# A graph layer with an expert layer behind it: chunks of a range summed together, an expert's first layer in pairs of blocks

## The chip, the cores and the metric

The kernel runs on one core of a Trainium2 chip. The time is the device time of one execution in microseconds (us); less is better. A core has engines that run side by side: TensorE (PE in the profile, with its weight loads as PEld), VectorE (DVE), ScalarE (ACT), GpSimd (POOL) and SyncE (SP), and 16 DMA engines. Each engine takes its own instructions in order; where one needs what another made, it waits for a semaphore.

## The reference

There are 6250 nodes with 256 features and 106,250 edges, sorted by their destination `dst`. Cut to what matters, it is

```python
deg = maximum(segment_sum(ones, dst), 1); norm = deg ** -0.5
# graph layer
h = norm * (layernorm(x) @ W.T + b)
x = x + segment_sum(h[src], dst) * norm
# expert layer, on the layernorm of the new x
scores = layernorm(x) @ Wg.T + bg              # 8 experts
top2, idx = top_k(scores, 2); p = softmax(top2)
for e in range(8):
    hid = relu(xn @ W1[e].T + b1[e])           # 256 -> 1024
    y = hid @ W2[e].T + b2[e]                  # 1024 -> 256
    x = x + combine[:, e] * y                  # combine holds p where idx is e
```

So every edge reads one row of 256 features at an address that is data, rows are summed by destination, and each node then goes through two of eight experts.

## The kernel before

**Start.** `gnn_ffn` (L1354) loads indices and x, and makes helper tiles. A value `bad` tells whether the edges are ordered well enough; L1422 loads it as `flag`, and `tc.If(flag == 0)` (L1423) runs `in_order`, its `Else` runs `any_order`. With the given data `in_order` runs. It first counts degrees and writes a table of scaled rows to memory (`ftable`, 128 rows at a time, each row 1 KB: a high and a low half in f16). This takes the first 93 us of the span.

**Main loop** (L816 to 832). The edges are 831 chunks of 128 (`NC`). A window is a run of successive chunks whose destinations lie within 128 nodes; there are 150, 110 of them of four or five chunks. Step s of the loop issues, for all engines, in this order:

- `gather(s + AHEAD)` (L391, DMA at L394): GpSimd starts an indirect DMA that brings the 128 source rows of a chunk six steps ahead (`AHEAD = 6`) into one of 24 buffers (`ROWS`).
- `mask(s + MASKS)` (L398, L401): VectorE makes a 128x128 matrix of ones and zeros that tells which edge goes to which node, six steps ahead, in one of nine buffers.
- `add_up(s)` (L403, L408): TensorE multiplies mask and rows (f16, 512 columns) and adds into the window's sum `ps` in PSUM (two buffers). It waits for the mask and for the row's DMA.
- The tasks planned for step s. `join(w)` (L474, L482 and L485 on VectorE, copies at L490 on ScalarE) adds the window's sum, one step after its last chunk, to what earlier windows left for the same nodes. A tile of 128 nodes is complete at step `FINAL[t]`, mostly 17 chunks after the one before. Then, at fixed steps counted from `s = FINAL[t] + 1`: `turn_sum` (s+2, L492), `linear` (s+4, L501, matmul at L505), `route` (s+5 and following, L508 to 599: residual at L513, layernorm, top two, softmax, positions `pos` at L592), `scatter` (L601, DMA at L603), which sends each row to the queues of its two experts by two indirect DMAs on GpSimd, at the positions that VectorE worked out. From s+16+LATE on `fetch`: `choose` (L618 to 657, VectorE) picks the expert with most rows waiting, `load_first` and `load_second` (L659 to 675) let SyncE load its weights (1152 and 1028 KB) and 256 of its rows.
- `next_piece(s)` (L792): one piece of the expert step that is on. There are 16 pieces of a full step of 256 rows: eight times `up` (L695 to 703: two matmuls in the code into `ph`, then ScalarE's relu with bias) and eight times `down` (L705 to 717: two matmuls into `py`; every fourth has VectorE add the bias, L715, and SyncE store the result). A second piece goes in at every fourth step when the experts are behind. `turn_rows` (matmuls at L690, copy at L692) brings the next step's rows into place.

The order is written out by hand (`tc.manual_schedule()`): each engine's queue holds its instructions in the order in which the loop names them. So GpSimd's scatters stand between its gathers, and a gather behind a scatter goes out only when VectorE has worked out where the scattered rows go.

In the trace each f32 matmul of the code is two records: `up` and `down` have four records a piece (1792 of L701 for 448 pieces, 1728 of L711 for 432).

**Tail** (L833 to 875). The remaining pieces, `read_back` (L773, indirect DMAs on GpSimd that bring each node's two results), `add_in` (L781) and stores. A last branch (L905) is for rows that no usual step took.

Of the kernel before, what the change touches and what calls it, by code (L numbers as in the profile page):

```python
# [19 lines left out]
P = 128  # L20
# [29 lines left out]
AHEAD = 6  # L50
UP = 2.0 ** 8
UP2 = 2.0 ** 11
MASKS = 6
ROWS = 24
# [44 lines left out]
BASE = [WINDOWS[w][0] for w in WINDOW]  # L99
FINAL = [max(chunks[-1] for n0, chunks in WINDOWS if n0 < (t + 1) * P) for t in range(NT)]  # L100
# [33 lines left out]
def in_order(ctx: ExitStack, tc: tile.TileContext, g: Shared):  # L134
# [240 lines left out]
    rows, masks, sums = {}, {}, {}  # L375
# [15 lines left out]
    def gather(c):  # L391
        nonlocal last_pool
        rows[c] = rowpool.tile([P, 2 * D], F16, name="rows")
        last_pool = nc.gpsimd.indirect_dma_start(  # L394
            out=rows[c], out_offset=None, in_=table[:, :],
            in_offset=bass.IndirectOffsetOnAxis(ap=g.src[:, c:c + 1], axis=0))

    def mask(c):  # L398
        masks[c] = work.tile([P, P], F16, name="mask", bufs=MASKS + 3)
        r = (P - BASE[c] % P) % P  # L400
        nc.vector.tensor_scalar(masks[c], g.col_b[:, r:r + P], g.rel[:, c:c + 1], None, op0=OP.is_equal)  # L401

    def add_up(c):  # L403
        w = WINDOW[c]
        chunks = WINDOWS[w][1]
        if c == chunks[0]:
            sums[w] = psp.tile([P, 2 * D], F32, name="ps")
        nc.tensor.matmul(sums[w], masks.pop(c), rows.pop(c), start=(c == chunks[0]), stop=(c == chunks[-1]))  # L408
# [37 lines left out]
    def inputs_scored(t0, t1):  # L446
        xT = turned_inputs.pop(t0)
        for t in range(t0, t1):
            px = psp.tile([P, NE], F32, name="ph")
            for k in range(2):  # L450
                nc.tensor.matmul(px, xT[:, k, (t - t0) * P:(t - t0 + 1) * P], wg[:, k, :],  # L451
                                 start=(k == 0), stop=(k == 1))
            nc.scalar.activation(xg[:, t, :], px, AF.Copy)
# [241 lines left out]
    def up(step, b):  # L695
        f = steps[step]
        w1 = f["w1"]
        n = rows_of(step)
        ph = psp.tile([P, FT], F32, name="ph")
        for k in range(2):  # L700
            nc.tensor.matmul(ph[:, :n], w1[:, k * H + b * P:k * H + (b + 1) * P], f["xT"][:, k, :n],  # L701
                             start=(k == 0), stop=(k == 1))
        nc.scalar.activation(f["hid"][:, b, :n], ph[:, :n], AF.Relu, bias=w1[:, 2 * H + b:2 * H + b + 1])  # L703

    def down(step, i):  # L705
        f = steps[step]
        a = i // 4
        if i % 4 == 0:
            f["py"] = psp.tile([P, D], F32, name="py")
        for b in (2 * (i % 4), 2 * (i % 4) + 1):  # L710
            nc.tensor.matmul(f["py"], f["hid"][:, b, a * P:(a + 1) * P], f["w2"][:, b * D:(b + 1) * D],  # L711
                             start=(b == 0), stop=(b == HB - 1))
        if i % 4 == 3:
# [6 lines left out]
        if i == 4 * rows_of(step) // P - 1:  # L720
            del steps[step]

# [36 lines left out]
    all_sent = FINAL[NT - 1] + 1 + 19  # L759
# [32 lines left out]
    def next_piece(s):  # L792
# [6 lines left out]
        if turned == step or (ahead and cur >= (12 if s < NC else 14)):  # L799
# [7 lines left out]
        if cur < HB:  # L807
            up(step, cur)
        else:
            down(step, cur - HB)  # L810
        cur += 1
        if cur == HB + 4 * rows_of(step) // P:
# [3 lines left out]
    with tc.manual_schedule():  # L816
        with rowp as rowpool:
            for c in range(AHEAD):
                gather(c)
            for c in range(MASKS):  # L820
                mask(c)
            for s in range(NC):
                if s + AHEAD < NC:
                    gather(s + AHEAD)
                if s + MASKS < NC:
                    mask(s + MASKS)
                add_up(s)
                for fn, args in tasks.pop(s, []):
                    fn(*args)
                next_piece(s)  # L830
                if s % 4 == 0 and earliest.get(done + 1, NC) <= s:
                    next_piece(s)
        with tc.tile_pool(name="ftail", bufs=2) as pool:  # L833
            s = NC
# [15 lines left out]
            while done < USUAL or tasks or len(plan) > 1 or asked < 2 * allowed or pend:  # L850
                for fn, args in tasks.pop(s, []):
                    fn(*args)
                if s > all_sent:
# [6 lines left out]
                    if loaded1 < min(chosen, done + (cur >= HB) + 3):  # L860
# [3 lines left out]
                next_piece(s)  # L864
# [26 lines left out]
            def more(step):  # L891

                some = some_left("some")
                with tc.If(nc.values_load(some[0:1, 0:1], min_val=0, max_val=1) > 0):
                    run(fetch(step))
                    turn_rows(step)
                    for b in range(HB):
                        up(step, b)
                    for i in range(8):
# [455 lines left out]
def gnn_ffn(ctx: ExitStack, tc: tile.TileContext, x, srcT, dstT, low, gW, gb, Wg, bg, W1, W2, out):  # L1355
# [67 lines left out]
    with tc.If(flag == 0) as cmp:  # L1423
        in_order(tc, g)
    with cmp.Else():
        any_order(tc, g, dstT)
# [43 lines left out]
```

## Time and profile before

| | |
|---|---|
| runs | 2164.18, 2155.74, 2160.90 us; median 2160.9 |
| profiled execution | 2166.43 us, of which the span in the profile is 2164.6 |
| mean granted TensorE clock | 0.803 |
| PE busy | 1379.5 us (64%), 6246 matmuls |
| DVE busy | 882.9 us (41%), 4681 instructions |
| ACT busy | 400.9 us (19%), 903 |
| POOL busy | 998.2 us (46%), 1082 |
| DMA | 320.09 MB, 148 GB/s; POOL's queue 20.8% and SP's 22.6% of the 16 engines' span |
| degrees and table | 0 to 93 us |
| main loop | 93 to about 1936 us, 2.2 us a step |
| tail | about 1936 us to the end |

Busy time is summed over an engine's instructions; issuing DMAs, waiting and branching don't count. A line of the groups gives source line, engine, operation, what it writes and reads, the count, busy time, the mean of one in ns, and the idle time of the engine just before, with what ended most of it. "remote" as a releaser is another core or a queue that the trace doesn't know; "issue" is time in which the engine waited for nothing that the profile shows.

### The profile page before, as it was taken

How to read it: one execution, taken by the hardware profiler on the slowest of the kernel's cores; microseconds unless marked ns; L12 is line 12 of the kernel's file. 1: busy time of each engine (PE TensorE's matmuls, PEld its weight loads, DVE VectorE, ACT ScalarE, POOL GpSimd, SP SyncE). 2: the span in 40 equal slices, each digit the busy share in tenths (PEclk: the TensorE clock that was granted, in tenths of full speed). 3: DMA queues.
4: the chain of work that ended last, by engine and by line, in shares of the span. 5: the costliest groups of instructions: out<-in, count | busy, mean ns of one | idle time of the engine just before them, and what ended most of it. 6: DMA issues, size and time to landing. Idle time of an engine off the chain costs nothing. (4 is left out here: it accounts for less than half of the span.)

```text
span 2164.6 us, 22195 instructions
## 1 busy us (share of the span) xinstructions
PE 1379.5 (64%) x6246; PEld 1001.8 (46%) x6246; DVE 882.9 (41%) x4681; ACT 400.9 (19%) x903; POOL 998.2 (46%) x1082
## 2 busy tenths in 40 slices
PE   5144557746677675665765766677576657577885
PEld 5033335534444454444544544445355435455664
DVE  8313434324435253443534335343343344344442
ACT  3511112111112121121211112111111112121222
POOL 1265463543544545354453544535454544414563
PEclk9996668877878788778877777878788868877898
DMA  5542253443343534344353443534353434526774
GB/s 202 203 157 77 61 174 108 153 144 103 133 156 113 174 114 162 118 136 152 111 166 117 147 143 112 176 109 157 130 173 117 168 128 152 206 93 219 235 252 164
DMA packets 116822, 320.09 MB, mean 148 GB/s; under 512 B 22388, under 2 KB 63560, under 8 KB 102344
## 3 DMA queue, kind: packets, MB, share of 16 engines
q1 hardware_dynamic: 64444, 175.27, 22.6%
q0 software_dynamic: 51568, 142.67, 20.8%
q8 instruction: 53, 0.87, 0.2%
q14 instruction: 89, 0.73, 0.1%
q10 hardware_dynamic: 668, 0.55, 0.1%
HBM read 269.01 MB, written 49.39 MB: 147 GB/s over the span
## 5 line engine op out<-in xcount | busy, mean ns | idle before, releaser
L394 POOL DMA_INDIRECT rows<-ftable,src x831 | 788.1, 948 | 260.1 <-issue 198.1
L711 PE MATMUL py<-w,hid 128*128 128x256 f32 x1728 | 529.7, 432 | 187.2 <-issue 157.9
L701 PE MATMUL ph<-xT,w 128*128 128x256 f32 (+1 forms) x1792 | 518.7, 424 | 160.4 <-ACT xT L692 97.7
L711 PEld LDWEIGHTS py<-w,hid 128*128 128x128 f32 x1728 | 368.2, 219 | 285.5 <-issue 185.2
L701 PEld LDWEIGHTS ph<-xT,w 128*128 128x128 f32 x1792 | 363.0, 215 | 268.9 <-ACT xT L692 117.7
L408 PE MATMUL ps<-rows,mask 128*128 128x512 f16 x831 | 355.7, 444 | 164.7 <-DMA rows<-ftable,src 59.0
L603 POOL DMA_INDIRECT fhq<-h,posi x98 | 98.0, 1000 | 731.8 <-DVE pos L592 533.2
L703 ACT ACTIVATE hid<-ph,w 128x256 f32<-128x256 f32 (+1 forms) x448 | 207.6, 465 | 628.4 <-PE ph L701 229.0
L401 DVE TENSOR_SCALAR mask<-col_b,rel 128x128 f16<-128x128 bf16 x831 | 203.3, 256 | 168.6 <-remote 73.5
L482 DVE SCALAR_TENSOR_TENSOR rolled<-rolled,keep,ps 128x256 f32<-128x256 f32 x149 | 71.2, 478 | 365.4 <-remote 160.7
L408 PEld LDWEIGHTS <-mask 128*128 128x128 f16 x831 | 92.8, 113 | 225.9 <-DVE rolled L485 78.2
L490 ACT ACTIVATE whole<-rolled 32x256 f32<-32x256 f32 (+2 forms) x156 | 64.6, 414 | 674.4 <-DVE rolled L485 621.5
L513 DVE SCALAR_TENSOR_TENSOR xr<-pt,norm,xr 128x256 f32<-128x256 f32 x49 | 23.6, 482 | 271.9 <-remote 162.1
L505 PE MATMUL pt<-gw,uT 128*128 128x264 f32 x196 | 65.6, 465 | 93.3 <-issue 55.8
L773 POOL DMA_INDIRECT yb<-fyq,rowat x98 | 94.2, 962 | 64.2 <-issue 22.3
L715 DVE TENSOR_TENSOR y<-py,w 128x256 f32<-128x256 f32 x108 | 45.5, 422 | 188.9 <-PE py L711 97.8
L505 PEld LDWEIGHTS pt<-gw,uT 128*128 128x128 f32 x196 | 41.0, 221 | 115.1 <-issue 66.3
L690 PE MATMUL px<-ident,xs 128*128 128x128 f32 x216 | 50.1, 356 | 47.4 <-issue 35.8
L451 PE MATMUL ph<-wg,xT 128*128 128x8 f32 x196 | 35.5, 307 | 67.0 <-ACT xT L443 44.4
L451 PEld LDWEIGHTS ph<-wg,xT 128*128 128x128 f32 x196 | 34.4, 259 | 83.7 <-ACT xT L443 55.1
L690 PEld LDWEIGHTS px<-ident,xs 128*128 128x128 f32 x216 | 37.9, 188 | 71.0 <-issue 56.0
L485 DVE SCALAR_TENSOR_TENSOR rolled<-ps,rolled 128x256 f32<-128x256 f32 x150 | 63.6, 424 | 5.2
(176 smaller groups left out, 1010.8 us busy)
## 6 DMA issues: line engine op xcount, KB each, us to landing
w<-in_W SPq DMA_DIRECT2D x56, 1152.0 KB
w<-in_W SPq DMA_DIRECT2D x56, 1028.0 KB
fyq<-y SPq DMA_DIRECT2D x108, 128.0 KB
xs<-fhq SPq DMA_DIRECT2D x52, 256.0 KB
rows<-ftable,src POOLq DMA_INDIRECT x831
fyq<-zero SPq DMA_DIRECT2D x28, 256.0 KB
out<-xr POOLq DMA_DIRECT2D x11, 512.0 KB
xr<-in_x SPq DMA_DIRECT2D x6, 896.0 KB
```

The costliest lines, as they stand in the source:

```text
L394: last_pool = nc.gpsimd.indirect_dma_start(out=rows[c], out_offset=None, in_=table[:, :], in_offset=bass.IndirectOffsetOnAxis(ap=g.src[:, ...
L401: nc.vector.tensor_scalar(masks[c], g.col_b[:, r:r + P], g.rel[:, c:c + 1], None, op0=OP.is_equal)
L408: nc.tensor.matmul(sums[w], masks.pop(c), rows.pop(c), start=(c == chunks[0]), stop=(c == chunks[-1]))
L451: nc.tensor.matmul(px, xT[:, k, (t - t0) * P:(t - t0 + 1) * P], wg[:, k, :], start=(k == 0), stop=(k == 1))
L482: nc.vector.scalar_tensor_tensor(new, rolled, keeps[kept[w]], ps[:, 0:D], op0=OP.mult, op1=OP.add)
L505: nc.tensor.matmul(pl, uT[:, k, :], gw[:, k, :], start=(k == 0), stop=(k == 1))
L603: s = nc.gpsimd.indirect_dma_start(out=hq[:, :], out_offset=bass.IndirectOffsetOnAxis(ap=ixs[t][:, j:j + 1], axis=0), in_=h2s[t], in_offse ...
L690: nc.tensor.transpose(px[:, k, a * P:(a + 1) * P], f["xs"][:, a, k * P:(k + 1) * P], g.ident)
L701: nc.tensor.matmul(ph[:, :n], w1[:, k * H + b * P:k * H + (b + 1) * P], f["xT"][:, k, :n], start=(k == 0), stop=(k == 1))
L703: nc.scalar.activation(f["hid"][:, b, :n], ph[:, :n], AF.Relu, bias=w1[:, 2 * H + b:2 * H + b + 1])
L711: nc.tensor.matmul(f["py"], f["hid"][:, b, a * P:(a + 1) * P], f["w2"][:, b * D:(b + 1) * D], start=(b == 0), stop=(b == HB - 1))
L773: r = nc.gpsimd.indirect_dma_start(out=yb, out_offset=None, in_=yq[:, :], in_offset=bass.IndirectOffsetOnAxis(ap=where[:, t, j:j + 1], axi ...
```

## The change

**Sums of a group.** A window's chunks are split into groups of at most five (`GATHERS`; 195 groups: 144 of four chunks, 51 of five). The rows of a group share a tile of five places, in six buffers (`ROWS = 6`); its masks share a tile, in three buffers. `add_up` now takes a whole group, one step after the group's last chunk, and its matmuls go from the last chunk to the first. `join` and all that is counted from `FINAL` come one step later.

**Masks.** `mask(s)` is made at step s, no longer six steps ahead, and waits until its chunk's rows have landed (`after`). The matmuls no longer wait for the rows' DMAs themselves (`free_order`), only for the masks. `AHEAD` goes from 6 to 8.

**Experts.** `up` takes two blocks: four matmuls into one PSUM tile of two halves, then two ScalarE operations. `down` takes four matmuls at a time. `next_piece` is called at even steps, and at s % 8 == 1 when behind, so that the rate of matmuls stays. `inputs_scored` gathers two tiles' scores in one PSUM tile and copies them at once. In the tail `next_piece` is called every second step, which starts at NC + 1.

**The other path apart.** `If`/`Else` becomes two `If`s, with `any_order` first.

```diff
-AHEAD = 6
+AHEAD = 8
-MASKS = 6
-ROWS = 24
+GATHERS = 5
+ROWS = 6
...
+def groups():
+
+    found = []
+    for n0, chunks in WINDOWS:
+        parts = -(-len(chunks) // GATHERS)
+        for i in range(parts):
+            found.append(chunks[i * len(chunks) // parts:(i + 1) * len(chunks) // parts])
+    return found
...
     def gather(c):
         nonlocal last_pool
-        rows[c] = rowpool.tile([P, 2 * D], F16, name="rows")
+        k, i = IN_GROUP[c]
+        if i == 0:
+            rows[k] = rowpool.tile([P, GATHERS, 2 * D], F16, name="rows")
         last_pool = nc.gpsimd.indirect_dma_start(
-            out=rows[c], out_offset=None, in_=table[:, :],
+            out=rows[k][:, i, :], out_offset=None, in_=table[:, :],
             in_offset=bass.IndirectOffsetOnAxis(ap=g.src[:, c:c + 1], axis=0))
+        landing[c] = last_pool
 
     def mask(c):
-        masks[c] = work.tile([P, P], F16, name="mask", bufs=MASKS + 3)
+
+        k, i = IN_GROUP[c]
+        if i == 0:
+            masks[k] = work.tile([P, GATHERS, P], F16, name="mask", bufs=3)
         r = (P - BASE[c] % P) % P
-        nc.vector.tensor_scalar(masks[c], g.col_b[:, r:r + P], g.rel[:, c:c + 1], None, op0=OP.is_equal)
-
-    def add_up(c):
-        w = WINDOW[c]
+        m = nc.vector.tensor_scalar(masks[k][:, i, :], g.col_b[:, r:r + P], g.rel[:, c:c + 1], None,
+                                    op0=OP.is_equal)
+        after(m, [landing[c]], "the rows are there")
+
+    def add_up(k):
+        w = WINDOW[GROUPS[k][0]]
         chunks = WINDOWS[w][1]
-        if c == chunks[0]:
+        if GROUPS[k][0] == chunks[0]:
             sums[w] = psp.tile([P, 2 * D], F32, name="ps")
-        nc.tensor.matmul(sums[w], masks.pop(c), rows.pop(c), start=(c == chunks[0]), stop=(c == chunks[-1]))
+        mine, theirs = masks.pop(k), rows.pop(k)
+        n = len(GROUPS[k])
+        for i in reversed(range(n)):
+            m = nc.tensor.matmul(sums[w], mine[:, i, :], theirs[:, i, :],
+                                 start=(GROUPS[k][0] == chunks[0] and i == n - 1),
+                                 stop=(GROUPS[k][-1] == chunks[-1] and i == 0))
+            free_order(m, [landing.pop(GROUPS[k][i])], "its mask was made after the rows had landed")
...
     def inputs_scored(t0, t1):
         xT = turned_inputs.pop(t0)
+        px = psp.tile([P, 2, NE], F32, name="ph")
         for t in range(t0, t1):
-            px = psp.tile([P, NE], F32, name="ph")
...
-            nc.scalar.activation(xg[:, t, :], px, AF.Copy)
+        nc.scalar.activation(xg[:, t0:t1, :], px[:, :t1 - t0, :], AF.Copy)
...
-    def up(step, b):
+    def up(step, i):
+
...
-        ph = psp.tile([P, FT], F32, name="ph")
-        for k in range(2):
-            nc.tensor.matmul(ph[:, :n], w1[:, k * H + b * P:k * H + (b + 1) * P], f["xT"][:, k, :n],
-                             start=(k == 0), stop=(k == 1))
-        nc.scalar.activation(f["hid"][:, b, :n], ph[:, :n], AF.Relu, bias=w1[:, 2 * H + b:2 * H + b + 1])
+        ph = psp.tile([P, 2, FT], F32, name="ph")
+        for j in range(2):
+            b = 2 * i + j
+            for k in range(2):
+                nc.tensor.matmul(ph[:, j, :n], w1[:, k * H + b * P:k * H + (b + 1) * P], f["xT"][:, k, :n],
+                                 start=(k == 0), stop=(k == 1))
+        for j in range(2):
+            b = 2 * i + j
+            nc.scalar.activation(f["hid"][:, b, :n], ph[:, j, :n], AF.Relu, bias=w1[:, 2 * H + b:2 * H + b + 1])
 
     def down(step, i):
+
         f = steps[step]
-        a = i // 4
-        if i % 4 == 0:
+        a = i // 2
+        if i % 2 == 0:
             f["py"] = psp.tile([P, D], F32, name="py")
-        for b in (2 * (i % 4), 2 * (i % 4) + 1):
+        for b in range(HB // 2 * (i % 2), HB // 2 * (i % 2 + 1)):
...
     for t in range(NT):
-        s = FINAL[t] + 1
+        s = FINAL[t] + 2
...
     for w, (n0, chunks) in enumerate(WINDOWS):
-        tasks.setdefault(chunks[-1] + 1, []).insert(0, (join, (w,)))
+        tasks.setdefault(chunks[-1] + 2, []).insert(0, (join, (w,)))
+    for k, chunks in enumerate(GROUPS):
+        tasks.setdefault(chunks[-1] + 1, []).insert(0, (add_up, (k,)))
...
-        if turned == step or (ahead and cur >= (12 if s < NC else 14)):
+        if turned == step or (ahead and cur >= pieces_of(step) - (2 if s < NC else 1)):
...
             for c in range(AHEAD):
                 gather(c)
-            for c in range(MASKS):
-                mask(c)
             for s in range(NC):
                 if s + AHEAD < NC:
                     gather(s + AHEAD)
-                if s + MASKS < NC:
-                    mask(s + MASKS)
-                add_up(s)
+                mask(s)
                 for fn, args in tasks.pop(s, []):
                     fn(*args)
-                next_piece(s)
-                if s % 4 == 0 and earliest.get(done + 1, NC) <= s:
+                if s % 2 == 0 or (s % 8 == 1 and earliest.get(done + 1, NC) <= s):
                     next_piece(s)
...
-                next_piece(s)
+                if s % 2 == 0:
+                    next_piece(s)
...
-    with tc.If(flag == 0) as cmp:
+    with tc.If(flag == 1):
+        any_order(tc, g, dstT)
+    with tc.If(flag == 0):
         in_order(tc, g)
-    with cmp.Else():
-        any_order(tc, g, dstT)
```

More of the change, by code (lines that the diff above doesn't have):

```diff
@@ L99 @@
 BASE = [WINDOWS[w][0] for w in WINDOW]
+def groups():
[5 more added lines that the diff above has]
+    return found
+GROUPS = groups()
+IN_GROUP = {c: (k, i) for k, chunks in enumerate(GROUPS) for i, c in enumerate(chunks)}
 FINAL = [max(chunks[-1] for n0, chunks in WINDOWS if n0 < (t + 1) * P) for t in range(NT)]
@@ L374, in in_order @@
     rowp = tc.tile_pool(name="frow", bufs=ROWS)
-    rows, masks, sums = {}, {}, {}
+    rows, masks, sums, landing = {}, {}, {}, {}
     h2s, ixs = {}, {}
@@ L447, in inputs_scored @@
         xT = turned_inputs.pop(t0)
+        px = psp.tile([P, 2, NE], F32, name="ph")
         for t in range(t0, t1):
-            px = psp.tile([P, NE], F32, name="ph")
             for k in range(2):
-                nc.tensor.matmul(px, xT[:, k, (t - t0) * P:(t - t0 + 1) * P], wg[:, k, :],
+                nc.tensor.matmul(px[:, t - t0, :], xT[:, k, (t - t0) * P:(t - t0 + 1) * P], wg[:, k, :],
                                  start=(k == 0), stop=(k == 1))
-            nc.scalar.activation(xg[:, t, :], px, AF.Copy)
+        nc.scalar.activation(xg[:, t0:t1, :], px[:, :t1 - t0, :], AF.Copy)
     def clear_results():
@@ L698, in up @@
         n = rows_of(step)
[L699 to L703 removed]
+        ph = psp.tile([P, 2, FT], F32, name="ph")
[7 more added lines that the diff above has]
+            nc.scalar.activation(f["hid"][:, b, :n], ph[:, j, :n], AF.Relu, bias=w1[:, 2 * H + b:2 * H + b + 1])
     def down(step, i):
         f = steps[step]
[L707 to L708 removed]
+        a = i // 2
+        if i % 2 == 0:
             f["py"] = psp.tile([P, D], F32, name="py")
[L710 removed]
+        for b in range(HB // 2 * (i % 2), HB // 2 * (i % 2 + 1)):
             nc.tensor.matmul(f["py"], f["hid"][:, b, a * P:(a + 1) * P], f["w2"][:, b * D:(b + 1) * D],
                              start=(b == 0), stop=(b == HB - 1))
[L713 removed]
+        if i % 2 == 1:
             y = work.tile([P, D], F32, name="y", bufs=4)
@@ L719, in down, with pieces_of @@
             writes.append((step, w))
-        if i == 4 * rows_of(step) // P - 1:
+        if i == 2 * rows_of(step) // P - 1:
             del steps[step]
+    UPS = HB // 2
+    def pieces_of(step):
+        return UPS + 2 * rows_of(step) // P
     tasks = {}
@@ L758, in in_order @@
     chosen = loaded1 = loaded2 = len(FOLLOWS)
-    all_sent = FINAL[NT - 1] + 1 + 19
+    all_sent = FINAL[NT - 1] + 2 + 19
     turned = 0
@@ L806, in next_piece @@
             return
-        if cur < HB:
+        if cur < UPS:
             up(step, cur)
         else:
-            down(step, cur - HB)
+            down(step, cur - UPS)
         cur += 1
-        if cur == HB + 4 * rows_of(step) // P:
+        if cur == pieces_of(step):
             done += 1
@@ L824, in in_order @@
                     gather(s + AHEAD)
-                if s + MASKS < NC:
-                    mask(s + MASKS)
-                add_up(s)
+                mask(s)
                 for fn, args in tasks.pop(s, []):
                     fn(*args)
-                next_piece(s)
-                if s % 4 == 0 and earliest.get(done + 1, NC) <= s:
+                if s % 2 == 0 or (s % 8 == 1 and earliest.get(done + 1, NC) <= s):
                     next_piece(s)
+            for fn, args in tasks.pop(NC, []):
+                fn(*args)
         with tc.tile_pool(name="ftail", bufs=2) as pool:
-            s = NC
+            s = NC + 1
             pend = []
@@ L859, in in_order @@
                         loaded2 += 1
-                    if loaded1 < min(chosen, done + (cur >= HB) + 3):
+                    if loaded1 < min(chosen, done + (cur >= UPS) + 3):
                         load_first(loaded1)
@@ L896, in more @@
                     turn_rows(step)
-                    for b in range(HB):
-                        up(step, b)
-                    for i in range(8):
+                    for i in range(UPS):
+                        up(step, i)
+                    for i in range(2 * FT // P):
                         down(step, i)
```

## The prediction

> **What bounds the kernel now.** I read the page's groups, then the list of waits, then busy time by stretches of two periods from the middle of the span, then the order of time on single engines there. The costliest groups name no engine that is full:
>
> ```profile
> L394 POOL DMA_INDIRECT rows<-ftable,src x831 | 788.1, 948 | 260.1 <-issue 198.1
> L711 PE MATMUL py<-w,hid 128*128 128x256 f32 x1728 | 529.7, 432 | 187.2 <-issue 157.9
> L701 PE MATMUL ph<-xT,w 128*128 128x256 f32 (+1 forms) x1792 | 518.7, 424 | 160.4 <-ACT xT L692 97.7
> L408 PE MATMUL ps<-rows,mask 128*128 128x512 f16 x831 | 355.7, 444 | 164.7 <-DMA rows<-ftable,src 59.0
> L603 POOL DMA_INDIRECT fhq<-h,posi x98 | 98.0, 1000 | 731.8 <-DVE pos L592 533.2
> L703 ACT ACTIVATE hid<-ph,w 128x256 f32<-128x256 f32 (+1 forms) x448 | 207.6, 465 | 628.4 <-PE ph L701 229.0
> L401 DVE TENSOR_SCALAR mask<-col_b,rel 128x128 f16<-128x128 bf16 x831 | 203.3, 256 | 168.6 <-remote 73.5
> ```
>
> The columns after the bar are busy us, mean ns of one, and idle us just before the group. POOL idles 731.8 us in front of 98 scatters, mostly for positions that VectorE computes. PE is 64% busy, DVE 41%. The stretches show how that comes about (columns: length, then busy us and count of PE, PEld, DVE, ACT, POOL, then clock, DMA share, GB/s):
>
> ```profile
> 998.60:1010.60 12.00, 11.77 (x53) 8.87 (x52) 4.88 (x32) 3.64 (x8) 9.24 (x10) 0.96 0.38 118
> 1010.60:1025.60 15.00, 4.20 (x16) 2.49 (x14) 0.00 (x0) 0.47 (x1) 8.87 (x10) 0.81 0.66 239
> 1025.60:1037.80 12.20, 8.63 (x26) 6.12 (x27) 10.88 (x56) 2.40 (x6) 0.00 (x0) 0.64 0.06 21
> 1037.80:1049.80 12.00, 9.72 (x40) 7.00 (x39) 4.96 (x32) 3.25 (x7) 9.23 (x10) 0.89 0.35 97
> 1049.80:1064.70 14.90, 8.27 (x28) 5.86 (x28) 0.00 (x0) 0.86 (x2) 8.89 (x10) 0.87 0.72 258
> 1064.70:1076.30 11.60, 9.41 (x32) 6.32 (x32) 10.80 (x57) 2.88 (x7) 0.00 (x0) 0.72 0.07 23
> 194.00:224.00 30.00, 3.59 (x13) 2.43 (x13) 1.77 (x6) 1.19 (x3) 19.96 (x22) 0.50 0.32 97
> ```
>
> A period (one tile of 128 nodes, mostly 17 chunks) lasts about 39 us. POOL sends some 20 indirect DMAs in a **burst**; DVE works in the first 12 us of it, then does nothing at all for 15 us (the **freeze**), then runs 89% busy for 12 us (the **catch-up**) while POOL has nothing to do. The seventh line is an early burst with a DMA share of 0.32: the freeze is there without the weight traffic. What ends it:
>
> ```profile
> 1021.27 0.95 POOL L394 DMA_INDIRECT rows<-ftable,src  x1 [0.30 <-issue]
> 1025.61 0.48 DVE L482 SCALAR_TENSOR_TENSOR rolled<-rolled,keep,ps 128x256 f32<-128x256 f32 x1 [15.03 <-remote]
> 1026.61 0.61 PE L408 MATMUL ps<-rows,mask 128*128 128x512 f16 x1 [4.67 <-DVE rolled L485]
> 1037.83 0.99 POOL L603 DMA_INDIRECT fhq<-h,posi  x1 [15.61 <-DVE pos L592]
> ```
>
> POOL's last gather ends at 1022.22, DVE moves 3.4 us later. L482 takes a sum whose last matmul PE had finished before 1011; it starts at 1025.61. So it waits for the news that the sum is there. In the same way ACT starts an L703 at 1014.35 after 6.7 us. I read this as signals between engines that arrive late while POOL's indirect DMAs run and earlier signals are still to be delivered. That is an inference: the profile shows who was late, not the signal.
>
> [...] L408 takes 0.38 us before the freeze and 0.61 after it, with the clock at 0.64. [...]
>
> **The change, part by part.** The sum is made against the profiled run: 2166.4 us, of which the span is 2164.6. It is 5.5 us above the median of the runs shown (2160.9), which I take off at the end.
>
> *Start and branch.* The other path becomes its own block ahead of this one: one more test on each engine. In the trace it is some 1 us from the flag to the first instruction. Either sign is open, 3 us at most: 0.
>
> *Gathers.* 831 gathers at 0.95 us and 0.30 of issue, 98 scatters at 1.3, stay: 831×1.25+98×1.3 = 1166 us, 23.6 a period. With eight instead of six ahead, POOL sends two more before it waits for a scatter. Since the sums come a step later, one of the two is lost again. Rows landed long before use (L408 waited only 59.0 us for them, 41.1 of it once), so nothing is gained: 0. A group's buffer is freed by one sum instead of chunk by chunk, but six groups hold 6×831/195 = 26 chunks (24 before): 0.
>
> *Masks.* 831×0.256 = 203 us of DVE stay. Each now waits for its row; behind it in DVE's order are the joins, the routing chain and so POOL's scatters. In the catch-up, rows of steps up to the scatter were sent in the burst before (POOL idles 12 us and more): that wait costs 0 there, and up to 1.4 us (a row's time from issue to landing in the stretch) at the first chunks if this cover goes. But the masks lose their **six steps of lead**, which is the dangerous part, priced under the rivals.
>
> *Sums.* 831 matmuls at 0.38 to 0.61 us stay, in 195 groups (144 of four chunks, 51 of five) that go without a break: PE's time is the same, but a row buffer, a mask and a sum are released 195 times instead of 831.
>
> *Up and down.* 448 blocks become 224 pairs: still 1792 and 1728 matmuls, still 448 ACT operations of 0.465 us, so 208 us of ACT stay. ACT's first of a pair starts after the second block (two matmuls' records of 0.42, about 0.9 us later): it is hidden, since the hidden block is first used several pieces later and ACT is 19% busy. The downs go from 432 pieces to 216. Pieces at every second step keep the rate. Scoring of inputs goes from 49 ACT copies to 25: 24×0.4 = 10 us of ACT at 19% busy, 0.
>
> *Signals.* Places where another engine waits on PE, counted in the code: sums 831, up 448, down 432 pieces (which free what they read), together 1711, 2.06 a step. After: 195, 224 to 448 and 216: 635 to 859, half or less. But a matmul that is inside a group still signals where a neighbour's wait needs it, and transposes, linear and scoring stay, so I take a third off, not a half. In the first 12 us of the burst at 998.6 PE did 9 sums, so 9×2.06 = 19 such signals before DVE stood. If the freeze begins when about as many have piled up, a third fewer a step lets 9/0.67 = 13 steps through instead of 9, if POOL's burst leaves time for them. At PE's pace there (12 us for 9) four steps need 5.3 us, and the freeze shrinks from 15 to about 10. I take **three of the four**. These steps leave the catch-up, where DVE needs 12.2 us for about 12 steps (56 instructions, 10.88 us busy): 1.03 us each. Gain 3×1.03 = 3.1 us a period. Between 93 us (degrees done) and 1936 us (last sums) there are 49 tiles; the first few fill the pipeline: 45 periods, 45×3.1 = 140 us.
>
> What is **late next**: DVE to PE, now tight. A fifth of the gain I give back for it (a mask of the last chunk must reach PE and the sum must come back before the next join): 140−28 = 112 us.
>
> *Tail.* From 1936 to 2165 us the chain of waits is PE's pieces, with stalls of 2.02, 5.36, 7.72, 6.49, 5.17, 4.38, 1.50, 2.46 and 3.30 = 38.4 us, the same freezes beside POOL's read-back. With a third fewer signals I take 11 us off. The tail starts one step later and pieces come in twos: +3.
>
> Sum: 2166.4 − 112 − 11 + 3 = 2046; less 5.5 is 2041, rounded to **2040 us**. Both ends of the uncertain term: zero to four steps of 1.03 to 1.2 us give 0 to 216 us.
>
> **The rivals.**
>
> *Freeze gone* (8%). If half the signals are below what the path can take, the period falls to POOL's 23.6 us plus the 3.4 us seen after its last gather, 27. 45×(39−27) = 540: about 1610 us. For it: in the first 12 us of each burst all ran at full pace. Against it: the burst's own signals are untouched, and in the seventh line above 30 us went by with 6 DVE instructions.
>
> *Freeze set by the DMAs themselves* (12%). POOL's 20 indirect DMAs a period are untouched, and if their completions are what clogs, PE's own signals don't matter; the change then doesn't do what it says. DVE still stands from the tenth DMA on: 2160 us, with the tail's few us lost in the noise.
>
> *Slower: the mask loop* (26%). Before, masks of six steps stood ready when a sum or a join was late, and PE could go on into the freeze (3 to 4 sums in it, by the same stretches). After, a group's last mask is issued after the join of the group before, in DVE's order, so each group needs sum to join to mask to sum: two crossings. With PE's other work between two groups (ten matmul records at 0.43 = 4.3 us) the loop hides until a crossing takes over about 1.5 us: 4.3 less the two join operations (0.9) and two masks (0.5), halved. From there it decides: at 0.7 us of excess a group, 4.3 groups a period, 3 us in each of 45 periods is +130, less 11 and 5 of the tail and the median: about 2265. Stretches with signals of 5 to 15 us speak for it; that the catch-up has short crossings speaks against it.
>
> **How the numbers follow.** Signals help as computed: 54%, own range 1960 to 2130; freeze gone 8%; unchanged 12%; mask loop 26%, 2180 to 2320. The range leaves out the first rival and the upper end of the last: 1890 to 2255. About 0.5% (11 us) is what a measurement of this kernel can tell from no change. Faster: 54+8 and part of the unchanged case, 0.65; same 0.08; slower 0.27.
>
> **What would show it.** In stretches of a period after: DVE's empty stretch nearer 10 than 15 us, over 40 DVE instructions before it, POOL's idle before the scatters near 620 instead of 732 us, catch-up some 9 us. The mask loop would show as PE L408 waiting for DVE mask, and L482 for PE, in the catch-up. The prediction is wrong if the freeze keeps its length (PE's signals weren't its cause), or if DVE's masks wait for rows for over 50 us.

## The result, and the profile after

The changed kernel takes 2198.3 us (median of four runs, 2190.4 to 2198.5) against 2162.5 us before (four runs): a ratio of 1.016, 95% interval 1.013 to 1.020. It is slower by some 36 us; the forecast was 2040. The profiled execution has a span of 2196.4 us, 31.8 more than the one before.

The groups that answer to those shown of before:

```profile
L410 POOL DMA_INDIRECT rows<-ftable,src x831 | 787.6, 948 | 270.0 <-issue 239.8
L433 PE MATMUL ps<-rows,mask 128*128 128x512 f16 x831 | 264.4, 453 | 601.5 <-DVE rh L554 325.9
L745 PE MATMUL py<-w,hid 128*128 128x256 f32 x1728 | 459.2, 417 | 51.8 <-issue 36.0
L732 PE MATMUL ph<-xT,w 128*128 128x256 f32 (+1 forms) x1792 | 428.4, 392 | 48.8 <-issue 21.0
L631 POOL DMA_INDIRECT fhq<-h,posi x98 | 99.6, 1016 | 737.5 <-DVE posi L617 627.1
L736 ACT ACTIVATE hid<-ph,w 128x256 f32<-128x256 f32 (+1 forms) x448 | 183.7, 462 | 400.7 <-PE ph L732 163.3
L421 DVE TENSOR_SCALAR mask<-col_b,rel 128x128 f16<-128x128 bf16 x831 | 198.8, 255 | 24.2 <-remote 15.9
```

POOL's idle time before the scatters is what it was: 737.5 us against 731.8. What moved is PE's waiting: in front of its sums (L433) it now stands for 601.5 us instead of 164.7, mostly for VectorE, and hardly any longer in front of the experts' matmuls (51.8 and 48.8 instead of 187.2 and 160.4). The wait has changed its place, and it isn't shorter: the three stand for 702.1 us together instead of 512.3, while their busy time fell from 1404.1 to 1152.0 us, for the same 4351 matmul records in longer unbroken runs.

One period of the changed kernel by stretches (columns as before): burst until the freeze, freeze, catch-up.

```profile
1024.20:1037.80 13.60, 10.66 (x51) 8.11 (x49) 7.22 (x40) 3.62 (x9) 10.55 (x11) 1.00 0.55 184
1037.80:1051.10 13.30, 0.00 (x0) 0.00 (x0) 0.00 (x0) 0.00 (x0) 7.62 (x9) 0.55 0.56 188
1051.10:1063.60 12.50, 11.15 (x44) 8.23 (x45) 8.88 (x49) 2.35 (x6) 0.03 (x1) 0.79 0.06 22
```

The freeze is still there. In this period it is total: PE, which before did 16 matmuls in the freeze at 1010.6 and 28 in the next, does none. Counted over 35 periods of each trace, PE does no matmul in VectorE's longest idle stretch in 13 of them, and in none before; the stretch itself lasts 12.1 us in the mean, and 12.4 before. The order of time around this freeze:

```profile
1031.24 3.62 PE L745 MATMUL py<-w,hid 128*128 128x256 f32 x16
1046.91 0.95 POOL L410 DMA_INDIRECT rows<-ftable,src  x1 [0.30 <-issue]
1051.13 0.42 DVE L749 TENSOR_TENSOR y<-py,w 128x256 f32<-128x256 f32 x1 [13.35 <-remote]
1051.77 1.46 PE L433 MATMUL ps<-rows,mask 128*128 128x512 f16 x3 [16.91 <-DVE rh L554]
```

PE ends the last matmul of an expert's result at 1034.86. L749, which reads just that, starts at 1051.13: 16.3 us later and 3.3 us after POOL's last gather of the burst (1047.86). The trace also keeps the times at which a semaphore was recorded as raised. The one that PE raises has records at 1036.23 and then at 1051.02, 1051.06 and 1051.10, the last 0.03 us before L749 starts. So it is the signal that comes late, which the prediction could only infer. Masks stand behind L749 in VectorE's order, and PE's sum stands behind the masks: one late signal now stops both engines.

The start is the other half. In the changed kernel:

```profile
9.38 0.13 DVE L1460 CAST pid<-pid_i 128x1 f32<-128x1 int32 x1
19.23 4.35 SPq L1431 DMA_DIRECT2D src<-in_srcT  x1
30.66 0.52 POOL L164 MEMSET zero<- 128x512 f32 x1 [29.09 <-SPq L1463]
30.71 0.93 DVE L173 CAST rel<-rel 128x831 int32<-128x831 f32 x1 [21.20 <-SPq L1463]
```

Before, both engines went on at once:

```profile
9.16 0.13 DVE L1420 CAST pid<-pid_i 128x1 f32<-128x1 int32 x1
9.84 1.01 DVE L159 CAST rel<-rel 128x831 int32<-128x831 f32 x1 [0.54 <-DVE pid L1420]
9.87 0.52 POOL L150 MEMSET zero<- 128x512 f32 x1 [8.30 <-DVE pid L1420]
```

L1463 is the first `If`, whose body is skipped. VectorE and POOL wait behind it for SyncE. SyncE issues loads of x and of the sources until 23.6 us, comes to the branch at 24.5 us, and then waits at the block's end for the semaphores of its loads one by one; the last load is recorded as landed at 30.06 us, and the two engines go on at 30.7. So they wait for loads to land, not only to be issued. Counted from the traces, the first gather goes out 20.2 us later than before, the last one 38.8 us later, and the end comes 31.8 us later: 20.2 at the start, 18.6 in the main loop, 7.0 given back in the tail.

### The profile page after: what moved, and what is told of

The parts are those of the page before. It is cut to its first block, busy times and chain, and to the rows that moved or that the text cites. A ratio compares the mean times of both kernels' runs of the same rounds, so it can differ in the third digit from the quotient of the medians.

```text
span 2196.4 us, 21456 instructions
## 1 busy us (share of the span) xinstructions
PE 1263.4 (58%) x6246; PEld 960.9 (44%) x6246; DVE 882.2 (40%) x4681; ACT 371.4 (17%) x879; POOL 999.0 (45%) x1082
## 5 line engine op out<-in xcount | busy, mean ns | idle before, releaser
L433 PE MATMUL ps<-rows,mask 128*128 128x512 f16 x831 | 264.4, 453 | 601.5 <-DVE rh L554 325.9
L745 PE MATMUL py<-w,hid 128*128 128x256 f32 x1728 | 459.2, 417 | 51.8 <-issue 36.0
L732 PE MATMUL ph<-xT,w 128*128 128x256 f32 (+1 forms) x1792 | 428.4, 392 | 48.8 <-issue 21.0
L631 POOL DMA_INDIRECT fhq<-h,posi x98 | 99.6, 1016 | 737.5 <-DVE posi L617 627.1
L433 PEld LDWEIGHTS <-mask 128*128 128x128 f16 x831 | 83.3, 110 | 719.7 <-DVE rh L554 334.1
L732 PEld LDWEIGHTS ph<-xT,w 128*128 128x128 f32 x1792 | 344.3, 201 | 108.4 <-issue 25.1
L749 DVE TENSOR_TENSOR y<-py,w 128x256 f32<-128x256 f32 x108 | 45.7, 424 | 526.7 <-remote 349.8
L736 ACT ACTIVATE hid<-ph,w 128x256 f32<-128x256 f32 (+1 forms) x448 | 183.7, 462 | 400.7 <-PE ph L732 163.3
L421 DVE TENSOR_SCALAR mask<-col_b,rel 128x128 f16<-128x128 bf16 x831 | 198.8, 255 | 24.2 <-remote 15.9
L533 PE MATMUL pt<-gw,uT 128*128 128x264 f32 x196 | 56.6, 415 | 27.2 <-ACT uT L526 25.2
L822 DVE SCALAR_TENSOR_TENSOR xr<-yb,prob,xr 128x256 f32<-128x256 f32 x98 | 45.6, 483 | 43.2 <-DMA yb<-fyq,rowat 26.3
L720 ACT ACTIVATE xT<-px 128x512 f32<-128x512 f32 (+1 forms) x56 | 32.1, 573 | 100.6 <-PE px L718 44.9
## 6 DMA issues: line engine op xcount, KB each, us to landing
w<-in_W SPq DMA_DIRECT2D x56, 1152.0 KB
```

The source lines that it names most:

```text
L421: m = nc.vector.tensor_scalar(masks[k][:, i, :], g.col_b[:, r:r + P], g.rel[:, c:c + 1], None, op0=OP.is_equal)
L433: m = nc.tensor.matmul(sums[w], mine[:, i, :], theirs[:, i, :], start=(GROUPS[k][0] == chunks[0] and i == n - 1), stop=(GROUPS[k][-1] == c ...
L533: nc.tensor.matmul(pl, uT[:, k, :], gw[:, k, :], start=(k == 0), stop=(k == 1))
L631: s = nc.gpsimd.indirect_dma_start(out=hq[:, :], out_offset=bass.IndirectOffsetOnAxis(ap=ixs[t][:, j:j + 1], axis=0), in_=h2s[t], in_offse ...
L732: nc.tensor.matmul(ph[:, j, :n], w1[:, k * H + b * P:k * H + (b + 1) * P], f["xT"][:, k, :n], start=(k == 0), stop=(k == 1))
L736: nc.scalar.activation(f["hid"][:, b, :n], ph[:, j, :n], AF.Relu, bias=w1[:, 2 * H + b:2 * H + b + 1])
```

## The experiments

The theory after the result had three parts: the split branch costs 21 us; the freeze is made by the density of POOL's indirect DMAs, not by the number of PE's signals, so the change left it alone; and masks without a lead make the rest. The rivals are the forecast's (fewer signals shorten the freeze) and that the longer pieces cause the loss.

In what follows the kernel before is run on the same chip each time, and ratios are to it. Chips differ: the kernel before took 2181, 2180 and 2159 us on three of them, which show freezes as in the profile, and 1467, 1463 and 1466 us on three others, where there are none. No run shows what makes the difference. I call them chips **with** and **without freezes** and compare only within a kind.

**One branch, and the split alone.** The edit is the last hunk of the change, undone in the changed kernel, and made alone in the kernel before.

> The changed kernel with If/Else as before. Theory (the branch): in the changed kernel POOL and DVE wait from 9.4 to 30.7 us behind the first If for SP, which is still sending loads of x; in the kernel before they went on at 9.8. Taking the split back gives about 20.9 us: 2198 - 21 = 2177 us, first gather near 93 us instead of 113. Rival (the branch costs nothing, x is loaded late anyway and what follows waits for it): 2195 to 2198 us.

> The kernel before with the two Ifs and nothing else. Theory (the branch): 2162 + 21 = 2183 us, first gather near 114 us. Rival: 2162 us, since the loads of x set when the degrees can be made.

With freezes. The split alone gives 1.0082 (1.0049 to 1.0115), some 18 us, and its first gather goes out 19.9 us later than before. The changed kernel with one branch gives 1.0122 (1.0067 to 1.0178): its first gather is back (0.4 us later than before), but a loss stays that is larger than expected. The ratio's interval just reaches the expected 1.0067, and it also holds the rival's 1.015 to 1.0165, so this run alone doesn't settle the branch. The split alone does, by its ratio and by the start of its trace. One thing came with the edit unasked. PE's instructions that raise a semaphore, counted in the traces, are 2757 in the kernel before and 907 in the changed one, but 2160 in the changed kernel with one branch, and 1978 in the kernel before with the split: without an `Else`, both kernels have fewer of them. So these two runs move the branch and the signals together.

**Pairs alone, groups alone.** The kernel before with `up`, `down` and `next_piece` of the changed one:

```diff
-                next_piece(s)
-                if s % 4 == 0 and earliest.get(done + 1, NC) <= s:
+                if s % 2 == 0 or (s % 8 == 1 and earliest.get(done + 1, NC) <= s):
                     next_piece(s)
...
```

> The kernel before with up in pairs, down in fours and pieces at every second step, sums and masks as before. Theory A (the sums and masks are what costs the main loop its 16 us): 2155 to 2165 us. Theory B (the longer pieces make PE answer later): about 2175 us. The forecast's theory (fewer signals from PE shorten the freeze): a third of its gain, about 2120 us.

And the changed kernel with one branch and the pieces of before:

> The kernel before with sums by group, masks at their own step behind the rows, AHEAD 8, pieces and If/Else as before. Theory A (the masks have lost their lead and DVE and PE wait for each other): 2172 to 2180 us, with PE L433's waits for DVE masks of some 200 us or more. Theory B (the pieces cost it): 2160 us. The forecast's theory: below 2100 us.

With freezes. Pairs alone: 1.0032 (1.0013 to 1.0050). Groups alone: 0.9976 (0.9958 to 0.9994). Neither part gives the loss by itself, and neither gives the forecast's gain. Together, in the changed kernel with one branch, they lose 1.2%. So the two act on each other. The wait that was expected with groups alone is there (L433 stands 241.3 us for masks), but it costs no time.

A table worked out from the traces shows how. Each line is a mean over 34 periods between 420 and 1800 us: period, POOL's burst, time from the burst's end to VectorE's first instruction over 2.2 us later (that threshold is mine), catch-up (all us), then PE's sums and matmul records until the catch-up and in it. The first two lines come from one chip, the other three from another, on which the kernel before took 19 us longer, so the parts are best compared with each other.

```
kernel            period  burst  resume  catch-up | sums      | matmuls
before             38.17  23.68   3.33    11.16   | 12.4  4.5 | 68.4 24.8
changed            38.94  23.67   3.26    12.00   |  9.5  7.4 | 57.1 36.1
... one branch     39.04  23.73   3.26    12.05   |  9.5  7.4 | 55.9 37.1
pairs alone        38.42  23.74   3.32    11.35   | 12.3  4.6 | 66.5 25.9
groups alone       38.27  23.77   3.27    11.23   |  9.4  7.5 | 56.8 36.6
```

Burst and resume together are 26.9 to 27.1 us in every line; only the catch-up moves. With groups and masks at their own step PE has eleven to twelve more matmuls to do in it than before. With the short pieces that costs nothing that shows in the time (0.998); with pieces twice as long between the sums a period is 0.8 us longer (39.04 us against 38.27, same chip). The trace of the changed kernel agrees: from the 300th to the 800th gather, some 30 periods, its lag grows from 16.7 to 38.8 us. That the long pieces do it by holding up the sums for the joins is argued from VectorE's share in the catch-up (busy 1.00 of it with groups alone, 0.96 with both; overlapping records count twice), not shown by a run of its own.

**What makes the freeze.** Three edits of the kernel before: `ROWS = 10`; a memset on POOL after each gather; rows of half the bytes.

```diff
-ROWS = 24
+ROWS = 10
```

> The kernel before with 10 row buffers instead of 24: POOL can be at most ten chunks ahead of PE's sums, so it can't send a tile's 17 gathers in one dense burst. Theory (a dense burst of indirect DMAs holds back the signals of the other engines until 3.3 us after its end): bursts are broken, the freezes get shorter or go, and the time falls clearly, to 1900 to 2100 us. Rival (what limits is the chain DVE positions to scatter to gathers, whatever the pitch): 2180 us, or slower by a few per cent, since gathers now wait for sums as well.

```diff
             in_offset=bass.IndirectOffsetOnAxis(ap=g.src[:, c:c + 1], axis=0))
+        nc.gpsimd.memset(filler, 0.0)
```

> The kernel before with a memset of 128x512 f32 on POOL after each gather (0.52 us each by the trace), so that gathers go out every 1.8 us instead of 1.25. Theory (density of the burst holds the signals): the freeze shrinks or goes, POOL's 17 to 19 DMAs take some 34 us a period and little is left behind it: 1850 to 2100 us. Rival (the burst holds the signals for as long as it lasts, at any pitch): the freeze grows by 10 us a period, 2181 + 45x10 = 2630 us.

```diff
-        rows[c] = rowpool.tile([P, 2 * D], F16, name="rows")
+        rows[c] = rowpool.tile([P, D], F16, name="rows")
...
-            out=rows[c], out_offset=None, in_=table[:, :],
+            out=rows[c], out_offset=None, in_=table.rearrange("n (h d) -> (n h) d", h=2),
...
```

> The kernel before with rows of 512 bytes instead of 1 KB, as many DMAs and rows: the gathers read half rows of the wrong places, and each sum takes the same half twice, so that the low halves of the table are left out. Theory (the number of rows or of DMA instructions holds the signals): freeze of 15 us as before, 2170 to 2185 us. Rival (the bytes or their writing to the buffers hold them): a shorter freeze, below 2100 us.

With freezes. Ten buffers: **0.797** (0.794 to 0.801), 1736.6 us. Paced: **0.846** (0.842 to 0.850), 1841.8 us, although POOL was given 453 us more of work. Half the bytes: 1.000 (0.997 to 1.003). So the gathers' bytes aren't it; pacing them or cutting their bursts is what helps. POOL's indirect DMAs without a pause over 0.6 us between them are 19 in a row in the kernel before (median) and 5 with ten buffers. Its groups there:

```profile
L394 POOL DMA_INDIRECT rows<-ftable,src x831 | 790.9, 952 | 438.8 <-issue 160.2 <-PE ps L408 109.5 <-remote 85.5
L603 POOL DMA_INDIRECT fhq<-h,posi x98 | 98.7, 1007 | 115.5 <-DVE pos L592 46.3 <-DVE upto L634 23.1 <-issue 18.3
```

Gathers now wait for PE's sums, and the scatters stand for 115.5 us instead of 731.8. The paced kernel's POOL, of the groups:

```profile
L395 POOL DMA_INDIRECT rows<-ftable,src x831 | 790.8, 952 | 154.3 <-issue 88.4
L398 POOL MEMSET filler<- 128x512 f32 x831 | 452.6, 545 | 0.3
L605 POOL DMA_INDIRECT fhq<-h,posi x98 | 98.1, 1001 | 46.7 <-DVE lf L630 17.2
```

A gather still takes 0.95 us, but POOL no longer waits for VectorE's positions: 46.7 us before the scatters instead of 731.8. By stretches, neither PE nor VectorE stands still in it:

```profile
900.00:913.20 13.20, 11.17 (x52) 7.95 (x50) 9.57 (x53) 4.99 (x11) 11.91 (x16) 1.00 0.46 127
913.20:928.00 14.80, 8.41 (x28) 6.34 (x28) 6.78 (x29) 0.42 (x1) 13.05 (x17) 0.84 0.64 234
928.00:944.00 16.00, 15.29 (x70) 11.41 (x69) 10.82 (x60) 6.21 (x14) 14.40 (x20) 0.94 0.34 92
```

The records of the semaphores tell whose signals are late. I counted those that stand over 2 us after the last instruction that raises the semaphore:

```
                              TensorE's       VectorE's     ScalarE's
before, with freezes          419 of 2445     10 of 3370    2 of 672
before, paced, with            15 of 2312      3 of 3127    2 of 734
changed, with freezes         158 of  802      3 of 2707    2 of 536
changed, without freezes        2 of  909      2 of 3423    2 of 658
```

Only TensorE's signals are late, and pacing nearly ends it. On chips with freezes some records are missing (TensorE raised the semaphore 2757 times in the kernel before), on the others hardly any. Why, and whether that belongs to the freeze, no run shows.

**The changed kernel paced, masks ahead, a smaller memset, pairs with ten buffers.** These four ran on a chip without freezes, so they answer other questions than those they were made for. The edit for the masks:

```diff
-        masks[k] = work.tile([P, GATHERS, P], F16, name="mask", bufs=3)
+        masks[k] = work.tile([P, GATHERS, P], F16, name="mask", bufs=4)
...
-                mask(s)
+                if s + 4 < NC:
+                    mask(s + 4)
...
```

> The changed kernel with one branch and with the same memset on POOL after each gather as in the paced kernel of before (ratio 0.846 to before). Theory (dense bursts hold the signals, and the change leaves the bursts as they are): the freeze goes here too, ratio 0.84 to 0.87. Theory of the mask loop (its cost shows in the catch-up at half clock, where PE is behind): with the freeze gone it costs nothing, so not over 0.85. Rival (the mask loop costs it 0.8 us a period at any time): 0.86 to 0.87.

> The changed kernel with one branch and masks made four steps ahead again, in four buffers of groups; still behind their rows. Theory (the masks' lead is what PE lacks in the burst, 9.5 sums there instead of 12.4, so that it has 36 matmuls to do in the catch-up instead of 25): PE gets to 11 or 12 sums in the burst, the catch-up goes from 12.0 to about 11.3 us, time 1.012 to about 1.003 of before. Rival (the groups' coarse sums and long pieces cost it, whenever the masks are made): 1.010 to 1.015.

> The paced kernel of before with a memset of half the size (128x256), so a pitch of about 1.4 us between gathers instead of 1.65 (paced) and 1.25 (before). If the delay of signals grows with what a gather leaves behind per unit of time and has a limit between 1.25 and 1.4, the freeze is gone and POOL's shorter period shows: about 26 to 28 us a period, 1700 to 1760 us. If the limit lies above 1.4, freezes are left: 1850 to 2100 us.

> Pairs of blocks and downs of four (as in the changed kernel) with sums by chunk, one branch and ten row buffers. With 10 buffers the kernel before is at 0.797 of its time. Theory (pairs cost only what a late signal makes of them): 0.79 to 0.80. If fewer signals from PE help once bursts are broken: 0.76 to 0.785. If PE's longer pieces delay the sums, on whose release the gathers now wait: 0.81 to 0.83.

Against 1467 us: 1.225 (1.222 to 1.229), 1.010 (1.007 to 1.013), 1.109 (1.105 to 1.112) and 1.002 (1.000 to 1.003). Pacing only costs where nothing freezes, since POOL's pitch then sets the time: at half pacing 831×1.44 + 98×1.3 makes 1324 us, and from the first gather to the last the trace has 1330 us. Nothing follows for the freeze. (The half clock that the first of these expectations names: in the changed kernel's catch-up at 1051.1 us the granted clock was 0.50 in the first 3.9 us, 0.68 in the next 2 and 1.00 in the last 6.6; in that of the kernel before at 1025.6 us it was 0.50 in the first 3.4 us.)

**Again, with the changed kernel itself and with eight row buffers.**

> The changed kernel as it is, once more, beside before on one chip. The last call's chip ran the kernel before in 1467 us, without freezes, three others in 2162 to 2181. On a chip with freezes: 1.012 to 1.020 of before. On one without: the branch's 20 us are 1.4%; the mask loop costs nothing where signals are quick, so 1.010 to 1.020 (about 1490 us); if the forecast's gain from fewer signals is there after all, below 1.0.

> The changed kernel with one branch and masks four steps ahead, on a chip that may have freezes. With freezes: if the lost lead costs the 0.8 us a period, PE gets to 11 or 12 sums in the burst and the time is 1.000 to 1.005 of before; if it was the coarse sums and long pieces, 1.008 to 1.014. Without freezes: 1.0097 again.

> The kernel before with the half memset after each gather (pitch 1.44 us). With freezes on this chip: if the limit of the held signals lies between 1.25 and 1.44, the time is that of the chip without them (1626 us), 0.74 to 0.76 of before; if above 1.44, 0.85 to 0.95. Without freezes: 1.11 again.

> The kernel before with 8 row buffers (10 gave 0.797 on a chip with freezes). With freezes: bursts of eight at most, so the last delays go, 0.76 to 0.79; if gathers begin to wait for sums, 0.80 to 0.85. Without freezes: 1.00 to 1.03, since there POOL's gathers set the period and now wait for sums.

Another chip without freezes (before 1463 us): changed 1.010 (1.008 to 1.013), masks ahead 1.009 (1.007 to 1.011), half pacing 1.109 (1.107 to 1.112), eight buffers 1.005 (1.003 to 1.006). The changed kernel is slower here too, by 15 us: what its branch costs less some 5 us, whose source I didn't isolate. Masks ahead, with one branch, starts its gathers 19.4 us earlier on the same chip and yet takes as long: 1179.1 us from the first gather to the last, against 1162.4. It makes the masks earlier and its TensorE raises the semaphore 2160 times instead of 907; which of the two costs the 17 us, no run tells apart. The changed kernel's stretches, at the same pitch of gathers as everywhere:

```profile
700.00:712.00 12.00, 11.25 (x54) 8.71 (x52) 9.46 (x53) 2.78 (x7) 8.95 (x11) 1.00 0.62 192
712.00:724.00 12.00, 8.99 (x44) 6.40 (x43) 6.57 (x36) 3.19 (x8) 9.26 (x10) 1.00 0.76 249
724.00:736.00 12.00, 11.97 (x58) 9.41 (x56) 8.72 (x49) 2.78 (x7) 8.95 (x11) 1.00 0.63 196
```

POOL sends without a stop, and VectorE is busy for 6.6 to 9.5 us of every 12. I measured in the traces how long after PE's last matmul a VectorE operation that had been idle for it starts (joins and results, 300 to 1200 us):

```
                              median   9 in 10 below   over 2 us
changed, without freezes       0.04        0.04          0 of  97
changed, with freezes          0.04       14.55         25 of 100
before, with freezes           0.04        9.01          9 of  47
before, ten buffers, with      0.04        5.30         23 of  98
```

The same program passes the same signals in 0.04 us on one chip and in up to 16 us on another. In the paced kernel, on a chip with freezes, the same count gives 0.04 us, with none of some 110 over 2 us.

**Masks ahead, twice more, and three buffers of groups.**

> The changed kernel with one branch and masks four steps ahead once more, for a chip with freezes (kernel before at 2160 to 2180 us). The lost lead costs it: PE at 11 or 12 sums in the burst, catch-up near 11.3 us, 1.000 to 1.005 of before. Coarse sums and long pieces cost it: catch-up stays at 12 us, 1.008 to 1.014. Without freezes: 1.009 again, and the question stays open.

> The changed kernel with one branch and masks four steps ahead. With freezes (before at 2160 to 2180 us): 1.000 to 1.005 if the lost lead costs the 0.8 us a period, 1.008 to 1.014 if the coarse sums and long pieces do. Without freezes 1.008 to 1.010, as three times now.

> The changed kernel with one branch, AHEAD 6 and three buffers of groups (12 to 15 chunks) instead of six. With freezes: bursts get shorter as with ten buffers in the kernel before (0.797), but release comes by the group, so 0.80 to 0.88. Without freezes: 0.995 to 1.03, since POOL's gathers set the period there and now wait for sums of groups.

The third time was again without freezes: 1.008 (1.006 to 1.010). The fourth was on a chip with them (before 2159 us): **0.982** (0.978 to 0.987), 2120 us. That is better than either value expected: with the long pieces the lost lead costs 3%, not 1% (1.0122 against 0.982, each to before on its own chip, so across two chips with freezes). With the short pieces its loss didn't show (groups alone, 0.998). In the table of periods:

```
... masks ahead    37.56  23.69   3.02    10.86   | 12.8  4.1 | 72.4 20.7
```

PE is back at 12.8 sums before the catch-up and has 20.7 matmuls left in it. The groups show the same (the changed kernel's L433 stood for 601.5 us):

```profile
L433 PE MATMUL ps<-rows,mask 128*128 128x512 f16 x831 | 254.9, 439 | 117.4 <-DVE rh L554 69.3 <-DVE mask L421 44.5 <-issue 3.6
```

The changed kernel with one branch, `AHEAD = 6` and `ROWS = 3`, on the same chip: 0.827 (0.823 to 0.831), 1783 us. It gains as the kernel before does from ten buffers: its gathers stand for 513.6 us, 182.0 of them for PE's sums (L433), instead of 270.0 us in the changed kernel. The length of its bursts wasn't counted. It stays behind ten buffers in the kernel before (0.797, another chip with freezes). That its buffers are freed by groups would explain it, but wasn't tested. That kernel is the fastest of all on chips with freezes; it wasn't run on one without, where eight buffers cost 0.5% and ten with pairs 0.2%.

## Why the prediction was wrong

**What bounds the kernel** was read rightly: the freeze, and signals that arrive after POOL's burst, are what pacing takes away, and the records of TensorE's semaphore show the signals late.

**The step that failed is "Signals".** It took the freeze to begin when a number of PE's signals has piled up, and let a third fewer signals pass four more steps, three of them as gain, 140 us. In the traces PE's signals fell by two thirds (2757 to 907), twice as much as I had assumed, and the freeze kept its length (12.1 us in the mean, 12.4 before) and its end: in most periods of both kernels VectorE resumes 3.2 to 3.4 us after POOL's last gather. Fewer signals from PE didn't shorten it; what did, on chips with freezes, was POOL sending less densely. The rival "Freeze set by the DMAs themselves" named this and got 12%. That POOL's DMAs and not the number of PE's signals set the freeze was right; that it is their completions that clog isn't shown. Its time (2160) was not right, because of the next two points. Even with masks ahead (2160 signals) the change gains 0.6 us a period where the sum had 3.1; whether fewer signals give that or the unbroken runs of matmuls, no run tells apart.

**"Start and branch"** had 0, at most 3 us. Measured 20.2 us at the first gather. The trace of before held the number: SyncE was issuing loads until 24.5 us there too, and nobody waited for it. I priced the branch's own instructions, and not that an engine with loads in flight has to arrive at it.

**The mask loop** was right in that the lost lead costs time, and its size was too large: 3 us a period, measured 0.8. It also sat elsewhere. I had it decide in every group, from crossings of 1.5 us on; it is paid once a period, when PE comes to the catch-up with 36 matmuls instead of 25, and only with the longer pieces (groups alone 0.998). Its sum was wrong too: 2166 + 130 − 11 − 5 is 2280, not 2265. That the measured 2198 lies within this rival's 2180 to 2320 is in good part luck, since 20 of the 36 us are the branch.

**"Gathers", "Masks" (waiting for rows) and "Up and down"** were put at nothing each. For rows VectorE's masks wait at most 24.2 us in all, 15.9 of it for an unknown releaser; the gathers' idle is 270.0 us against 260.1; pairs alone cost 0.3%. Right within some 10 us. (A period of POOL's own work is 1166/49 = 23.8 us, not 23.6; nothing hangs on it.)

**The tail** had −11+3 us; measured −7.0. This can be luck: the −11 rests on the same failed step, and from the last gather to the end the changed kernel with one branch takes 2.6 us less than before, the kernel before with the split 11 us more.

The sum against the profiled run of before: 2164.6 + 20.2 + 18.6 − 7.0 = 2196.4 us. The direction was wrong because the signals' story got 54% without anything in the trace that told PE's signals from POOL's bursts as the cause. The two stretches spoke against it: PE does only 16 and 28 matmuls in the 15 us of freeze, after 53 and 40 in the 12 us ahead of it, so few signals are added, and yet VectorE stands until 3.4 us after POOL's last gather.

## What to carry to other kernels

When several engines stand still together and all resume a fixed time after one engine's burst (here 3.0 to 3.3 us in the mean), change that burst first (fewer buffers, or something between its instructions): here one constant was worth 20% on chips with freezes, where the reworked sums, masks and pieces were worth 2% at best. Where there were no freezes a like one (eight row buffers) cost 0.5%, so measure on the chip that counts. At the end of a skipped block, here, VectorE and GpSimd waited until 30.7 us for SyncE and its loads: before splitting a branch, look for the engine that is latest there. And a lead that an engine has over another (masks six steps ahead) can let the other work through a stall; here it was worth 3% with freezes and long pieces, and without freezes no gain from it showed.

## What the runs showed of the hardware

- Dense indirect DMAs from GpSimd (0.95 us each, 1.25 us apart, 19 in a row) went with signals from TensorE to VectorE up to 16 us late, on three of the six chips of the experiments; at 1.65 us apart the freezes were gone (none of some 110 signals over 2 us late), and with bursts cut by ten buffers the delay fell from 9.0 to 5.3 us (nine in ten below). On the other three chips gathers at the same pitch go with quick signals: 0.04 us in the changed kernel. What happens between 1.25 and 1.65 us is open: the kernel at 1.44 us only met chips without freezes.
- Of the semaphores that TensorE, VectorE and ScalarE raise, only TensorE's rose late on chips with freezes: 419 of 2445 records over 2 us in the kernel before, against 10 of 3370 of VectorE's and 2 of 672 of ScalarE's.
- At the end of a skipped block SyncE waited until its loads had landed (30.06 us), and VectorE and GpSimd went on 0.6 us later.
- The kernel before took 1463 to 1467 us on the three chips without freezes, and 2159 to 2181 on the others. A time is worth little without the kernel before on the same chip.
- The memset on POOL slowed VectorE's masks: 391 ns each in the changed kernel (273 without it, both on chips without freezes), and 402 in the kernel before (256, both on chips with them). I don't take such slowing for the freeze: a gather took 948 to 955 ns in every kernel, with freezes and without, and in the freezes at 1010.6 and 1037.8 us VectorE ran nothing at all.
